# Seven products of 512 x 512 weights in two recurrent layers, each written as seven block products

## The chip, the cores and the metric

The kernel runs on one core of one Trainium2 chip. The time is the time of one execution on the device in microseconds (us). A core has five engines with queues of their own: TensorE (PE in the profile; PEld is its weight load), VectorE (DVE), ScalarE (ACT), GpSimd (POOL) and SyncE (SP), which issues most transfers (DMAs) between the memory of the chip (DRAM) and the core's on-chip memory. That on-chip memory is SBUF, 128 partitions wide, and PSUM, where TensorE puts its products, in banks of 128 x 512 numbers.

## What is computed

Four layers are applied in turn to x of shape (8, 112, 512): a cross attention (layer 0), two recurrent layers (1 and 2), and a layer with two attentions and an MLP (layer 3); layers 0 and 3 attend to a context of shape (8, 375, 512). All numbers are float32. The change lies in layers 1 and 2. Cut to what matters, layer 1 is:

```python
xa = _ln(x, ln1_w, ln1_b)
...                                     # r, k, v, g, w from mixes of xa and its shift by one token
def step(s, inp):
    k_l, v_l, w_l, r_l = inp
    a = k_l[..., :, None] * v_l[..., None, :]
    out = jnp.einsum('bhs,bhst->bht', r_l, faaaa * a + s)
    s_new = a + w_l[..., None] * s
    return (s_new, out)
_, outs = jax.lax.scan(step, s0, seq)   # over 112 tokens
y = outs.transpose(1, 0, 2, 3)
...                                     # group norm of y over each head
x = x + y * g @ Wo.T                    # time mix: the product called o
xc = _ln(x, ln2_w, ln2_b)
sxc = jnp.concatenate([state[:, i0][:, None], xc[:, :-1]], axis=1) - xc
xk2 = xc + sxc * fmaa_k
xr2 = xc + sxc * fmaa_r
rr = jax.nn.sigmoid(xr2 @ fWr.T)        # the product called fr
kk = jnp.square(jax.nn.relu(xk2 @ fWk.T))   # fk
x = x + rr * (kk @ fWv.T)               # channel mix: fv
```

Layer 2 has the same form, with weights Wfk, Wfr and Wfv. Everything in front of o is called the time mix, everything behind it the channel mix. All weights named here are 512 x 512.

## The kernel before

Activations lie transposed: 128 channels on the partitions, four channel blocks c, and 896 tokens along the row (8 sequences of 112), worked on in two halves h of 448 tokens. A tile of one activation is 128 x 4 x 896.

A product of such a tile with a weight is written in two ways:

- `project` (matmul at L167) makes, for each half h and each output block o, four matmuls of 128 x 128 by 128 x 448 over the four input blocks: 2 x 4 x 4 = 32 matmuls of 448 columns. In the profile one such matmul is two records. The function that is handed in takes each finished bank.
- `seven` (matmul at L1162) splits weight and activation into 2 x 2 blocks (two input and two output halves of 256 channels; two input halves by two token halves) and makes seven block products in place of eight: 7 x 2 input blocks x 2 output blocks m = 28 matmuls of 448 columns. It needs four sums of weight quarters (`weight_sums`, 128 x 512 each) and four sums of token blocks (`token_sums`, 128 x 896 each). Its parts have the names k1 to k8 in the tile names: k1 and k2 for both m first, and then for each m k6, k7, k5, k4 and k8, where k4 adds on to k7's bank and k8 to k5's. ACT copies k1 out (p1), DVE adds it to k6 (u2) and u2 to k7 (u3), and each output block is a bank plus u2 or u3. Layer 3 uses it for its queries, outputs and MLP, where the page calls its banks ps_k1q, ps_k6fc and so on.

In layers 1 and 2 the products o, fk, fr and fv go through `project`. Layer 3's keys and values do not depend on x. They are computed in layers 1 and 2 as a filler: `values()` hands out pieces (matmuls at L994), and `fill(n)` puts n pieces into PE's queue at places chosen by hand. ACT copies a piece out of PSUM (L1019, L1092, L1106), POOL adds parts together (L1020), SP loads the context's blocks (L978) and stores the result (L1010 to L1014), and POOL prepares sums of layer 3's value weights (L910 to L913, L930, L932).

The scan of the time mix (`time_mix`, L626) runs over 4 channel blocks of 16 steps each, 64 steps a layer, in this order: ACT copies v, spread to the partitions, into the PSUM buffer vp (L666, L667), DVE multiplies it by k into the PSUM buffer kv (L765), DVE scans with the decay into st (L769), POOL multiplies by r into rs (L773), and PE sums over the partitions (L746) when enough rs are there. vp and kv have one buffer each. The sums of a finished block are added to v's place (`take`, L712), which is now y, and its group norm (`group_norm`: reciprocals L699, POOL multiplies at L701 and, with the gate g, at L707) runs beside the scan of the next block; that of the last block runs behind the loop, beside filler. Then comes o, whose result is added to x by DVE (L794).

Inside the loop the order of the instructions on each engine is the order of the text (`tc.manual_schedule`). Around it, and in the channel mix, a scheduler chooses the order from dependencies, and may move an instruction that is written behind the loop into an engine's queue among the loop's.

The channel mix (L797) makes the shifted difference sxc (`shifted`, POOL, L437 and L438), mixes xk2 and xr2 from it (DVE, L819), and has `squared` as the end of fk (ACT relu L834, DVE square L835), a sigmoid on ACT at the end of fr (L844), and `add` at the end of fv (DVE product L850, POOL add L851). In layer 2, fv's second half of tokens is interleaved with layer 3's first LayerNorm.

## Time and profile before

| | us |
|---|---|
| three runs | 2889.84, 2891.95, 2893.08 |
| median | 2891.95 |
| profiled execution | 2892.85 |
| its span | 2890.7 |
| PE busy (97% of the span) | 2791.5 |
| DVE busy (62%) | 1800.7 |
| POOL busy (36%) | 1052.2 |
| ACT busy (35%) | 1012.7 |
| granted clock of PE, mean | 0.989 |

Times in the trace count from the start of the span; the execution's own time is 2.15 us more than the span. The scan loop of layer 1 runs from about 344 to 605, that of layer 2 from about 961 to 1226. o runs from 625 and from 1258, the channel mix's products from 697 to 767 and from 1344 to 1416. Busy shares are means over stages with different limits: the scan loops keep DVE and POOL busy as well as PE, the channel mixes keep PE alone busy.

An instruction's line in the timeline gives its start, its length, its engine, its line of the program, the operation, the tiles out<-in, the shapes and, in brackets, how long the engine was idle before and what released it. The chain of waits is the work that ended last, followed back from the end.

### The profile page before, as it was taken

What the parts mean: (1) busy time and instruction counts of PE and PEld (TensorE: products, weight loads), DVE (VectorE), ACT (ScalarE), POOL (GpSimd) and SP (SyncE); (2) the same over time, 40 slices, a digit from 0 to 9 for tenths busy, and PEclk for the clock granted to TensorE, in tenths of its full rate; (3) what the DMA queues carried; (4) which work ended last, traced back from release to release, by engine and by line L of the source; (5) the groups of instructions that cost most, each with busy time, mean ns of one, the idle gap of its engine ahead of it and who ended that gap; (6) DMA issues with size and microseconds to landing.
All of it is one profiled execution on the core that took longest, in us unless ns stands there. A gap on an engine that the chain in (4) does not pass through costs nothing.

```text
span 2890.7 us, 31049 instructions
## 1 busy us (share of the span) xinstructions
PE 2791.5 (97%) x10476; PEld 1588.2 (55%) x10476; DVE 1800.7 (62%) x2301; ACT 1012.7 (35%) x1953; POOL 1052.2 (36%) x836
## 2 busy tenths in 40 slices
PE   8989999999999999999999999999899999999999
PEld 4734443344444433347467676767476676767544
DVE  1464288856352688834457676757767676757555
ACT  2232466633243456523233232313333232313311
POOL 1432178744231487733322221313122232313030
PEclk9999999999999999999999999999999999999999
DMA  5621498944221789842435352525244352523010
GB/s 206 239 77 39 142 282 254 277 122 136 85 71 57 236 241 277 241 137 92 130 103 156 95 165 94 163 92 159 74 133 133 115 166 89 162 93 115 28 47 26
DMA packets 233310, 400.90 MB, mean 139 GB/s; under 512 B 35144, under 2 KB 170344, under 8 KB 226368
## 3 DMA queue, kind: packets, MB, share of 16 engines
q1 hardware_dynamic: 233152, 398.92, 44.1%
q8 instruction: 84, 1.38, 0.2%
q14 instruction: 74, 0.61, 0.1%
HBM read 321.06 MB, written 77.91 MB: 138 GB/s over the span
## 4 chain that ended last, share of the span: by engine, by line
PE 73%; DVE 15%; POOL 4%; ACT 4%; issue 2%; DMA 2%; SPq 0%; DVEq 0%; ACTq 0%; POOLq 0%
PE ps_vk L994 14%; PE ps_k1k L1235 8%; PE ps_k5k L1235 6%; PE av L1496 4%; PE sc L1448 4%; PE ps_o L167 3%; DVE each L1488 2%; PE ps_k1q L1162 2%; PE ps_fk L167 2%; PE ps_r L562 2%; PE ps_k L562 2%; PE ps_k5q L1162 2%; PE ps_k7q L1162 2%; PE ps_v L562 2%; PE ps_fr L167 2%
## 5 line engine op out<-in xcount | busy, mean ns | idle before, releaser
L994 PE MATMUL ps_vk<-wv,cv 128*128 128x512 f32 x1296 | 583.8, 601 | 15.4 <-ACT k L1092 9.1
L994 PEld LDWEIGHTS ps_vk<-wv,cv 128*128 128x128 f32 x1296 | 243.5, 191 | 339.8 <-issue 285.4
L1483 POOL PARTITION_ALL_REDUCE each<-tops x113 | 182.4, 1614 | 466.0 <-DVE tops L1472 464.1
L1020 POOL TENSOR_TENSOR k<-k,k 128x512 f32<-128x512 f32 (+1 forms) x153 | 197.8, 1293 | 327.0 <-ACT k L1019 276.4
L1458 POOL PARTITION_ALL_REDUCE tops<-top x128 | 139.3, 1088 | 427.5 <-DVE top L1456 417.3
L769 DVE TENSOR_TENSOR_SCAN st<-decay,kv 128x904 f32<-128x904 f32 x128 | 260.7, 2037 | 17.6 <-POOL rs L773 4.4
L773 POOL TENSOR_TENSOR rs<-st,r 128x896 f32<-128x896 f32 x128 | 247.3, 1932 | 51.6 <-DVE st L769 46.7
L1466 ACT ACTIVATE pts<-pts,rests 128x448 f32<-128x448 f32 (+1 forms) x256 | 133.2, 567 | 337.6 <-DVE pts L1464 325.9
L1496 PEld LDWEIGHTS av<-pts,v 125*128 125x128 f32 (+1 forms) x1536 | 190.9, 191 | 33.1 <-ACT pts L1466 3.9
L1448 PEld LDWEIGHTS sc<-q,k 128*128 128x128 f32 x1536 | 189.4, 192 | 33.0 <-DVE each L1488 9.4
L1448 PE MATMUL sc<-q,k 128*128 128x112 f32 x1536 | 193.0, 276 | 8.6 <-DVE each L1488 8.3
L1488 DVE RECIPROCAL each<-each 128x224 f32<-128x224 f32 x113 | 174.7, 1546 | 31.3 <-POOL each L1483 28.7
L1496 PE MATMUL av<-pts,v 125*128 125x112 f32 (+1 forms) x1536 | 190.9, 274 | 1.3 <-ACT pts L1466 1.3
L1235 PE MATMUL ps_k1k<-cs,wsk 128*128 128x375 f32 x480 | 173.6, 483 | 6.5 <-ACT u2k L1237 5.3
L765 DVE TENSOR_TENSOR kv<-vp,k 128x904 f32<-128x904 f32 x128 | 141.5, 1105 | 60.5 <-ACT vp L667 55.3
L1019 ACT COPY k<-ps_vk 128x512 f32<-128x512 f32 (+1 forms) x153 | 89.2, 583 | 179.6 <-PE ps_vk L994 176.8
L1092 ACT COPY k<-ps_vk 128x512 f32<-128x512 f32 (+1 forms) x153 | 89.1, 583 | 172.9 <-PE ps_vk L994 163.7
L1456 DVE TENSOR_REDUCE top<-sc 128x224 f32<-128x672 f32 x128 | 109.1, 852 | 28.6 <-PE sc L1448 28.6
L667 ACT COPY vp<-vj 128x896 f32<-128x896 f32 x124 | 112.8, 910 | 9.3 <-DMA vj<-rows 5.4
L1464 DVE TENSOR_TENSOR pts<-sc,tops 128x672 f32<-128x672 f32 x128 | 102.8, 803 | 17.6 <-POOL tops L1458 17.6
L1235 PEld LDWEIGHTS ps_k1k<-cs,wsk 128*128 128x128 f32 x480 | 84.0, 189 | 51.3 <-ACT u2k L1237 7.6
L1237 ACT COPY p1k<-ps_k1k 128x375 f32<-128x375 f32 x60 | 27.9, 465 | 212.1 <-PE ps_k1k L1235 212.1
(416 smaller groups left out, 4788.6 us busy)
## 6 DMA issues: line engine op xcount, KB each, us to landing
vj<-rows SPq DMA_DIRECT2D x124, 448.0 KB
cv<-blocks SPq DMA_DIRECT2D x181, 251.5 KB
cs<-blocks SPq DMA_DIRECT2D x120, 375.0 KB
wvs<-k SPq DMA_DIRECT2D x128, 256.0 KB
v<-wvs SPq DMA_DIRECT2D x128, 256.0 KB
cx<-in_ctxT SPq DMA_DIRECT2D x38, 750.0 KB
v<-wvs SPq DMA_DIRECT2D x128, 126.0 KB
wvs<-k SPq DMA_DIRECT2D x64, 224.0 KB
```

What stands on the lines that cost most here:

```text
L167: nc.tensor.matmul(p, w[:, k, o * P : (o + 1) * P], rhs(k, h), start=k == 0, stop=k == NC - 1)
L562: nc.tensor.matmul(y, ws[f][:, c, o * P : (o + 1) * P], x_f, start=c == 0, stop=c == NC - 1)
L769: nc.vector.tensor_tensor_scan(flat(st), flat(decay[:, c]), flat(kv), 0.0, ALU.mult, ALU.add)
L773: nc.gpsimd.tensor_mul(by_batch(rs), st[:, :, :L], by_batch(r[:, c, :]))
L994: nc.tensor.matmul(to, left, right, start=start and n == 0, stop=k == 1, skip_group_check=True)
L1020: nc.gpsimd.tensor_add(y, z, y)
L1162: nc.tensor.matmul(to, lhsT, rhs, start=start and k == 0, stop=k == 1, skip_group_check=not start)
L1235: nc.tensor.matmul(y, lhsT, rhs, start=start and k == 0, stop=k == 1, skip_group_check=True)
L1448: nc.tensor.matmul(sc[:, t, y * L : (y + 1) * L], kt[:, o, t * CT : t * CT + P], q[:, o, b * L : (b + 1) * L], start=True, stop=True,)
L1483: nc.gpsimd.partition_all_reduce(each, it[4], P, ReduceOp.add)
L1488: nc.vector.reciprocal(each, sums)
L1496: nc.tensor.matmul(av[:, y], v[:nt, t, y * HD : (y + 1) * HD], pts[:nt, t, y * L : (y + 1) * L], start=t == 0, stop=t == 2,)
```

## The change

o in both layers, fk and fr in both layers, and fv in layer 1 go from `project` to `seven`. fv of layer 2 stays.

- `weight_sums`, `token_sums`, `seven` and their helpers move up, so that layers 1 and 2 can call them. `seven` gets a switch `whole`, which writes k4 ahead of k5, and takes a function for the places of p1, u2 and u3.
- For o, the weight sums are made by DVE in the tile k, and the token sums by DVE in the tile r, in pieces of 128 x 448 (`sums_of_tokens`); the text has the calls behind the loop, in the last block's group norm. p1, u2 and u3 lie in the tile decay.
- For the channel mix, POOL makes the weight sums, in rr (fk), in sxc (fr), in sxc and xk2 (fv). DVE makes three token sums of 128 x 896 each and POOL the fourth. p1, u2 and u3 lie in a tile that LayerNorm has used before (tag "half"). xr2 has no tile any more: the mix is written over xc. A tile tx2 is new.
- fk's end becomes a DVE add (where there is u), a relu and a square on ACT. fr's gets a DVE add ahead of the sigmoid, fv's a DVE add ahead of the product, and o's second addend is added to x separately.

```diff
+    def weight_sums(pool, tag, w, u, eng=None, later=None):
...
+        a11, a12, a21, a22 = (w[:, k : k + 2, o : o + 256] for o in (0, 256) for k in (0, 2))
+        eng = eng or nc.gpsimd
+        steps = [
+            lambda: eng.tensor_add(y[0], a21, a22),
+            lambda: eng.tensor_sub(y[1], y[0], a11),
+            lambda: eng.tensor_sub(y[2], a11, a21),
+            lambda: eng.tensor_sub(y[3], a12, y[1]),
+        ]
+        if later is not None:
+            later.extend(steps)
+            return y
+        for step in steps:
+            step()
+        return y
+    def token_sums(eng, b11, b21, b12, b22, t):
+        eng.tensor_sub(t[:, 0], b12, b11)
+        eng.tensor_sub(t[:, 1], b22, t[:, 0])
+        eng.tensor_sub(b12, b22, b12)
+        eng.tensor_sub(t[:, 2], b21, t[:, 1])
+    def seven(ps, work, w, s, b, t, n, put, u, whole=False):
...
+        first, p1 = [], []
+        for m in range(2):
+            first.append(bank("k1", m))
+            product(first[m], m, lambda k: w[:, k], b11)
+            p1.append(tile_of("p1", m))
+            nc.scalar.copy(p1[m], first[m])
+            yield
+        for m in range(2):
+            product(first[m], m, lambda k: w[:, 2 + k], b21, start=False)
+            put(0, m, first[m], None)
+            yield
+        for m in range(2):
+            p = bank("k6", m)
+            product(p, m, lambda k: s()[1][:, k], t[1])
+            u2 = tile_of("u2", m)
+            nc.vector.tensor_add(u2, p, p1[m])
+            yield
+            p = bank("k7", m)
+            product(p, m, lambda k: s()[2][:, k], t[2])
+            u3 = tile_of("u3", m)
+            nc.vector.tensor_add(u3, p, u2)
+            yield
+            if whole:
+                product(p, m, lambda k: w[:, 2 + k, 256:], t[3], start=False)
+                put(0, 2 + m, p, u2)
+                yield
+            q = bank("k5", m)
+            product(q, m, lambda k: s()[0][:, k], t[0])
+            put(1, 2 + m, q, u3)
+            yield
+            if not whole:
+                product(p, m, lambda k: w[:, 2 + k, 256:], t[3], start=False)
+                put(0, 2 + m, p, u2)
+                yield
+            product(q, m, lambda k: s()[3][:, k], b22, start=False)
+            put(1, m, q, u2)
+            yield
+    def places(room, at, shapes):
+        room, ys = flat_all(room), []
+        for shape in shapes:
+            n = math.prod(shape)
+            y = room[:, at : at + n]
+            ys.append(y.rearrange("p (a b) -> p a b", b=shape[-1]) if len(shape) == 2 else y)
+            at += n
+        return ys
+    def temporaries(room, at=0):
+        a, b, c, e = places(room, at, [(NH,)] * 4)
+        given = {"p1": (a, b), "u2": (c, a), "u3": (e, e)}
+        return lambda what, m: given[what][m]
+    def quarters(y):
+        return [halves(y[:, k : k + 2], h) for h in range(2) for k in (0, 2)]
...
+            s_o = places(k, 0, [(2, 256)] * 4)
+            t_o = places(r, 0, [(2, NH)] * 3)
+            b11, b21, b12, b22 = quarters(y)
...
+            def sums_of_tokens(ks):
+                t0, t1, t3 = t_o
+                for k_ in ks:
+                    if not k_:
+                        for j in range(2):
+                            nc.vector.tensor_sub(t0[:, j], b12[:, j], b11[:, j])
+                    nc.vector.tensor_sub(t1[:, k_], b22[:, k_], t0[:, k_])
+                    nc.vector.tensor_sub(b12[:, k_], b22[:, k_], b12[:, k_])
+                    nc.vector.tensor_sub(t3[:, k_], b21[:, k_], t1[:, k_])
             last = group_norm(NC - 1, gate(NC - 1))
             for at in range(11):
                 next(last, None)
+                if not at:
+                    weight_sums(None, s_o, w_o, f"o{n}", nc.vector)
+                    sums_of_tokens([0])
                 fill(int(n == 2 or at % 2))
+            sums_of_tokens([1])
             banks.close()
             ps = banks.enter_context(tc.tile_pool(name=f"so{n}", bufs=6, space=PSUM))
-            def add(o, h, p):
-                xs = halves(x[:, o, :], h)
-                nc.vector.tensor_add(xs, p, xs)
-            project(ps, w_o, lambda c, h: halves(y[:, c, :], h), add, f"o{n}")
+            t0, t1, t3 = t_o
+            for _ in seven(
+                ps, temporaries(decay), w_o, lambda: s_o, (b11, b21, b22), (t0, t1, b12, t3), NH, add_to_x(None), f"o{n}", True
+            ):
+                pass
...
-            def mixed(maa, name):
-                y = one.tile([P, NC, N], F32, name=name)
+            def mixed(maa, y):
...
-            def squared(o, h, p):
+            def squared(h, o, p, u):
                 y = halves(kk[:, o, :], h)
+                if u is not None:
+                    nc.vector.tensor_add(y, p, u)
+                    p = y
                 nc.scalar.activation(y, p, AF.Relu)
-                nc.vector.tensor_mul(y, p, y)
-            xk = mixed(names["fk"], f"xk2_{n}")
-            project(ps, f_k, lambda c, h: halves(xk[:, c, :], h), squared, f"fk{n}")
-            xr = mixed(names["fr"], f"xr2_{n}")
-            project(
-                ps,
-                f_r,
-                lambda c, h: halves(xr[:, c, :], h),
-                lambda o, h, p: nc.scalar.activation(halves(rr[:, o, :], h), p, AF.Sigmoid),
-                f"fr{n}",
-            )
+                nc.scalar.activation(y, y, AF.Square)
+            def opened(h, o, p, u):
+                y = halves(rr[:, o, :], h)
+                if u is not None:
+                    nc.vector.tensor_add(y, p, u)
+                    p = y
+                nc.scalar.activation(y, p, AF.Sigmoid)
+            def sums_of(y, t):
+                b11, b21, b12, b22 = quarters(y)
+                t0, t1, t3 = t
+                nc.vector.tensor_sub(t0, b12, b11)
+                nc.vector.tensor_sub(t1, b22, t0)
+                nc.gpsimd.tensor_sub(b12, b22, b12)
+                nc.vector.tensor_sub(t3, b21, t1)
+                return (b11, b21, b22), (t0, t1, b12, t3)
+            def seven_of(w, s, y, t, put, u):
+                b, t = sums_of(y, t)
+                room = work.tile([P, NC, NH], F32, tag="half", name=f"parts_{u}")
+                weight_sums(None, s, w, u)
+                for _ in seven(ps, temporaries(room), w, lambda: s, b, t, NH, put, u, True):
+                    pass
+            xk = one.tile([P, NC, N], F32, name=f"xk2_{n}")
+            tx = one.tile([P, NC, N], F32, name=f"tx2_{n}")
+            s_k, s_r = (places(y, 0, [(2, 256)] * 4) for y in (rr, sx))
+            t_k, t_r = (places(y, 0, [(2, NH)] * 3) for y in (tx, xk))
+            mixed(names["fk"], xk)
+            seven_of(f_k, s_k, xk, t_k, squared, f"fk{n}")
+            mixed(names["fr"], xc)
+            seven_of(f_r, s_r, xc, t_r, opened, f"fr{n}")
...
+            def add7(h, o, p, u):
+                if u is not None:
+                    y = work.tile([P, NH], F32, tag="rstd", name=f"fvs{n}_{o}_{h}")
+                    nc.vector.tensor_add(y, p, u)
+                    p = y
+                add(o, h, p)
             if n == 1:
-                project(ps, f_v, lambda c, h: halves(kk[:, c, :], h), add, f"fv{n}")
+                s_v = places(sx, 2048, [(2, 256)] * 3) + places(xk, 2688, [(2, 256)])
+                seven_of(f_v, s_v, kk, t_k, add7, f"fv{n}")
```

## The prediction

> **What bounds the kernel now.** I read the page's busy shares and the engine shares of the chain first: TensorE (PE) is busy for 97% of the span. A microsecond of PE work saved is then a microsecond of time, if what feeds PE keeps up.
>
> ```profile
> PE 2791.5 (97%) x10476; PEld 1588.2 (55%) x10476; DVE 1800.7 (62%) x2301; ACT 1012.7 (35%) x1953; POOL 1052.2 (36%) x836
> PE 73%; DVE 15%; POOL 4%; ACT 4%; issue 2%; DMA 2%; SPq 0%; DVEq 0%; ACTq 0%; POOLq 0%
> ```
>
> The chain in order of time gives the price of the products that the change touches: PE waits for nothing inside them, and one matmul (two records) takes 24.05 / 32 = 0.75 us.
>
> ```profile
> 625.26 24.05 PE ps_o L167 x64
> ...
> 718.69 24.05 PE ps_fr L167 x64
> 742.74 24.07 PE ps_fv L167 x64
> ```
>
> The table by stretches (each "time, (instructions)" pair is PE, PEld, DVE, ACT, POOL) shows a stretch of the MLP, where products already run as seven blocks, beside a plain product and a stretch of the second scan loop.
>
> ```profile
> 2803.00:2824.00 21.00, 21.00 (x57) 10.64 (x56) 6.20 (x11) 5.67 (x9) 1.21 (x1) 1.00 0.11 45
> ...
> 718.00:742.00 24.00, 24.00 (x65) 12.14 (x64) 2.01 (x3) 7.53 (x11) 0.00 (x0) 1.00 0.12 44
> ...
> 1155.00:1224.00 69.00, 66.96 (x204) 27.39 (x202) 61.11 (x40) 40.25 (x75) 55.53 (x37) 1.00 0.84 243
> ```
>
> Seven blocks fill PE too (21.00 of 21.00). In the scan loop PE idles 2.04 of 69 us while DVE (61.11) and POOL (55.53) are nearly full: there, added DVE work has little room.
>
> **Part 1, fewer products.** Seven products fall from 32 matmuls to 28: 4 x 0.75 = 3.0 us each, 21.0 us in all, on the path. The extra adds from PSUM (0.62 us each) come at most five to a group of 7.5 us of PE work, as in the MLP: hidden.
>
> **Part 2, o's sums enter the scan loop.** In the built order of the changed kernel DVE does not take them behind the loop, where it sits idle for 12.37 us ahead of the reciprocals at 620.01. It takes four weight sums and five of the token sums in each layer between the loop's multiplies (kv) and scans. Three of those places wait for POOL's gate multiply of a finished channel block; the kv or scan behind waits along, then the vp copy on ACT (one PSUM buffer), then the filler's copies on ACT, whose banks PE needs. In the timeline of layer 2's last place (columns: start, us, engine):
>
> ```profile
> 1217.44 1.11 DVE L765 TENSOR_TENSOR kv<-vp,k 128x904 f32<-128x904 f32 x1
> 1218.65 2.04 DVE L769 TENSOR_TENSOR_SCAN st<-decay,kv 128x904 f32<-128x904 f32 x1
> 1220.90 1.11 DVE L765 TENSOR_TENSOR kv<-vp,k 128x904 f32<-128x904 f32 x1 [0.21 <-ACT vp L667]
> ...
> 1220.00 1.16 POOL L707 TENSOR_TENSOR v<-v,gate 128x448 f32<-128x448 f32 x1
> ...
> 1226.28 1.69 PE L746 MATMUL ps_y<-rs,pick 128*32 128x448 f32 x10 [1.02 <-POOL rs L773]
> ```
>
> The scan of 1218.65 now stands behind a sum that waits for the gate until 1221.16: it starts at 1221.8. Two more sums (1.2) put the last kv at 1225.1, its scan at 1226.3 to 1228.3, POOL's rs at 1228.4 to 1230.3 in place of 1226.2. PE already waits for it at 1226.28, so all 4.1 us count. Layer 1's last place:
>
> ```profile
> 598.63 1.14 POOL L707 TENSOR_TENSOR v<-v,gate 128x448 f32<-128x448 f32 x1
> ...
> 598.89 1.11 DVE L765 TENSOR_TENSOR kv<-vp,k 128x904 f32<-128x904 f32 x1 [0.15 <-ACT vp L667]
> ...
> 602.84 1.93 POOL L773 TENSOR_TENSOR rs<-st,r 128x896 f32<-128x896 f32 x1
> ...
> 604.82 1.69 PE L746 MATMUL ps_y<-rs,pick 128*32 128x448 f32 x10 [1.57 <-POOL rs L773]
> ```
>
> Gate until 599.77, three sums of 0.62, kv at 601.6, scan 602.8 to 604.85, rs at 604.85 instead of 602.84: 2.0 us.
>
> The sums may take longer than 0.62. Two inputs from SBUF, beside a busy POOL:
>
> ```profile
> 683.25 11.42 DVE L819 SCALAR_TENSOR_TENSOR xk<-sxc,vecs,xc 128x448 f32<-128x448 f32 x8
> 694.59 6.87 DVE L819 SCALAR_TENSOR_TENSOR xr<-sxc,vecs,xc 128x448 f32<-128x448 f32 x8
> ```
>
> The same operation takes 1.43 us each while POOL works without a pause (680.99 to 693) and 0.86 beside two POOL adds. The kv and scan rows, with one input in PSUM, keep 1.11 and 2.04 whatever POOL does. If each sum stands behind the POOL operation that is then running, the first one of layer 1 starts at 601.67, after an rs: 3.9 us there, and in layer 2 an add until 1222.4 and an rs until 1227.0 make 7.2. I take a middle: 3.0 (2.0 to 3.9) and 5.5 (4.1 to 7.2).
>
> [...]
>
> The four earlier places, by the same reading:
> - Layer 1, kv of 468.39: the gate ends at 472.38, kv starts at 473.0, 4.6 late. POOL is behind there (its next rs for this block starts only at 477.76), so the scans' sums are not later. But the vp copy of 469.99 waits until 474.1, and the filler's copies on ACT behind it with it; PE has one product of 1.72 us in hand and gives back 0.7 that it idled at 479.75: 4.1 - 1.7 - 0.7 = 1.7 (0 to 4.6).
> - Layer 1, second place: kv of 534.51 goes to 536.0, less than a product: 0.3 (0 to 1.5).
> - Layer 2, kv of 1086.35: gate until 1089.18, kv 3.5 late, vp copy 2.7 late, less one product: 1.0 (0 to 3.5).
> - Layer 2, scan of 1154.22: gate until 1156.71, 3.1 late: 0.9 (0 to 3.1).
>
> The eight weight sums (0.6 each) fall between scans, where DVE has short idle times: 1.0 (0 to 4.8). Part 2 together: 13.4 us (6.1 to 28.6).
>
> **Part 3, o itself.** Its last gate multiply (630.56) is done by about 631.3, k6 starts 8 matmuls after 625.2, at 631.2; five adds to x are 3.1 us in 7.5: nothing (0 to 1).
>
> **Part 4, the channel mixes.**
> - fk of layer 1: DVE's mixing of xk ends at 694.6; three sums of 1.1 and eight mixes of 0.67 end at 703.3, or at 709 with a POOL operation ahead of each of four. Of fk's records 58 ran from 696.89; k1 and k2 would end at 700.6, k6 at 702.1, k7 and k5 at 705.1, and k4 cannot start before u3, two adds behind k6 on DVE: 1.5 (0 to 5).
> - fr's sums on DVE stand between the adds of fk's second half, two of 1.1 us ahead of adds that PE waits for: 0.7 in each layer, 1.4 (0 to 5).
> - fr of layer 1: on POOL seven weight sums (1.27 each) and the four wv sums (705.08 to 714.7 before, 2.35 each) now stand ahead of the token sum that k7 reads; 704 + 8.9 + 9.4 + 1.9 = 724.2, while k7 starts at about 725: 0.5 (0 to 3).
> - fk of layer 2: POOL's four weight sums of fr wait for the mixing and stand ahead of the filler's last four adds (L1020, 1334.09 to 1344.93); ACT has two buffers for these, and PE's pieces of 1339 to 1344 can wait: 1.0 (0 to 4).
> - Entry to layer 2: four POOL adds close together at fv's end, yet the load of Wv that the chain shows from 766.83 on starts some 3 us earlier against that end: 0 (-1 to 2).
> - ACT does the square: eight operations of 0.54 us more in each layer; ACT has 7.53 us of work in the 24 of 718 to 742: nothing (0 to 1, if its copies of p1 come late). No DMA is added.
>
> Part 4: 4.4 (-1 to 19).
>
> **Sum.** -21.0 + 13.4 + 0 + 4.4 = -3.2. The profiled run took 2892.85 (span 2890.7 and 2.15 around it), 0.90 above the median of 2891.95: 2889.65 for such a run, 2888.75 at the median, so 2889.
>
> **Rivals.** A measurement of this kernel tells 0.2% (5.8 us) from no change: the runs before spread over 3.2 us.
> - Absorbed: the loop's delays vanish in PE's own idle time (3.95 us of 1024 to 1090, 2.04 of 1155 to 1224) and in part 4 nothing shows. For it: DVE idles 3.52 at 1086.35, just where a sum goes. Against it: the last places end in a PE that already waits. -21 + 6.1 + up to 3 gives 2877 (2871 to 2880).
> - Slower, by one mechanism: sums with two SBUF inputs collide with POOL wherever they stand. At the last places that is 3.9 + 7.2, at the earlier ones one operation of POOL (1.3 to 1.9) ahead of each, some 4 x 1.5 more on the 3.9 taken, 8 weight sums at 1.4 rather than 0.6 (6), and the upper values for both fk, 9. Together 21.0 - 36 = 15 over; it decides from about 27 us of loss. 2898 to 2907. For it: the 11.42 us row. Against it: rows beside a sparse POOL (0.86).
> - The loop costs as in my sum, but the channel mixes wait for their sums, mostly the POOL queue ahead of k7 and the filler's adds: 10 to 19 instead of 4.4, 2894 to 2903.
>
> That seven blocks do not save 3.0 us each is hardly open, with 21.00 of 21.00 in the MLP.
>
> **Numbers.** My sum, with 2880 to 2897 as its own range: 0.37 (half of it under 2886.2). Absorbed 0.23, collisions 0.28, late sums 0.12 (about half within 0.2%). Faster 0.18 + 0.23 = 0.41, same 0.19 + 0.07 = 0.26, slower 0.28 + 0.05 = 0.33. The range reaches from the middle of the absorbed case to inside the collisions: 2874 to 2904.
>
> **What will show it.** Seven groups of 56 records at 21.0 us instead of 64 at 24.05; in the loops DVE sums that wait for POOL's gate multiplies, the scans behind them late, and PE waits for the last rs of 3 to 8 us instead of 1.57 and 1.02; sums of 128x448 longer than 0.62 where POOL is busy; PE gaps ahead of k4 in fk and k7 in fr. I am wrong if the stretches of the scan loops keep their length, or if a gap of over 5 us stands somewhere else, ahead of layer 2's first LayerNorm above all.

## The result: slower by 34.5 us, and the profile after

The changed kernel takes 2925.40 us (median of four runs, 2924.47 to 2931.13) against 2890.89 us of the kernel before on the same chip (four runs, 2889.32 to 2893.08). The ratio is 1.0121 with a 95% interval of 1.0109 to 1.0133: slower by 34.5 us. The prediction was 2889 (2874 to 2904). The profiled execution is the slowest of the four: 2931.13, with a span of 2929.0, 38.3 over the 2890.7 of before. All stage times below are from that execution.

The busy shares and the engine shares of the chain on the page of the changed kernel:

```profile
PE 2790.1 (95%) x10420; PEld 1585.8 (54%) x10420; DVE 1893.2 (65%) x2394; ACT 1029.4 (35%) x1983; POOL 1101.9 (38%) x861
PE 69%; DVE 17%; POOL 5%; ACT 4%; issue 3%; DMA 2%; SPq 1%; DVEq 0%; POOLq 0%; ACTq 0%
```

PE has 56 records fewer (28 matmuls of 0.75 us, 21 us), but its busy time falls by 1.4 us only, and its mean granted clock falls from 0.989 to 0.982: matmuls have become longer elsewhere. DVE has 92.5 us more to do and POOL 49.7. Their shares of the chain went up from 15% to 17% and from 4% to 5%.

Where the 38.3 us arise is read by putting the starts and ends of the same instructions of both profiles side by side. The table gives the offset of after against before at each mark, and what each stretch added:

| mark (time in before, us) | offset | the stretch up to it |
|---|---|---|
| first scan of layer 1 (347.08) | +2.32 | nothing is changed here |
| last scan of layer 1 (600.10) | +15.15 | scan loop: +12.83 |
| o starts (625.09) | +17.47 | rs, PE's wait, last block: +2.32 |
| o ends (649.31) | +16.30 | o as seven: -1.17 |
| fk starts (685.37) | +17.07 | LayerNorm: +0.77 |
| fk ends (718.69) | +23.97 | fk as seven: +6.90 |
| fr ends (742.74) | +21.26 | fr as seven: -2.71 |
| fv ends (766.80) | +19.98 | fv as seven: -1.28 |
| first scan of layer 2 (965.22) | +23.98 | entry to layer 2: +4.00 |
| last scan of layer 2 (1222.11) | +37.47 | scan loop: +13.49 |
| o starts (1258.12) | +39.03 | as above: +1.56 |
| o ends (1282.33) | +36.03 | o as seven: -3.00 |
| fk starts (1319.98) | +38.16 | LayerNorm: +2.13 |
| fk ends (1365.99) | +43.17 | fk as seven: +5.01 |
| fr ends (1390.04) | +40.17 | fr as seven: -3.00 |
| end (2890.74) | +38.25 | fv of layer 2, layer 3: -1.92 |

The two time mixes up to o cost 30.2 us, the two fk 11.9 where 6.0 were to be saved, the entry to layer 2 4.0. Only o of layer 2 and fr bring their 3 us. fv's blocks run without a pause as well, but 1.72 us of filler stand among them now.

The chain of waits of the changed kernel at the end of layer 1's loop (start, length, engine, tile, line):

```profile
605.46 1.92 POOL rs L914
607.38 1.23 POOL k L1206
608.61 1.10 POOL v L845
...
609.73 2.33 DVE r L933
612.05 1.62 DVE v L934
613.67 0.53 DVE r L935
614.20 1.03 DVE kv L906
...
615.25 2.05 DVE st L910
...
617.47 1.92 POOL rs L914
...
619.43 3.19 PE ps_y L887 x10
```

This is the row to compare with before's 598.63 to 604.82. POOL's gate multiply (L845) comes behind an rs and a filler add. Three token sums of o (L933 to L935) wait for it in DVE's queue, and the layer's last kv and scan stand behind them. On the chain two of the sums take 2.33 and 1.62 us, the third 0.53. PE waits 6.25 us for the last rs (1.57 in before). The same place in layer 2, in the timeline (in brackets the idle time before, and what ended it):

```profile
1252.13 1.67 DVE L933 TENSOR_TENSOR r<-v,r 128x448 f32<-128x448 f32 x1 [2.62 <-POOL v L845]
1256.19 2.33 DVE L935 TENSOR_TENSOR r<-v,r 128x448 f32<-128x448 f32 x1
1263.75 3.19 PE L887 MATMUL ps_y<-rs,pick 128*32 128x448 f32 x10 [4.72 <-POOL rs L914]
```

PE had idled 1.92 us just before that, so 6.6 us in all (1.02 in before). And what follows such a pause is slow as well. The table by stretches (time, then PE, PEld, DVE, ACT and POOL busy with their instructions, then the granted clock of PE, the DMA share and GB/s) shows the time behind three of the pauses:

```profile
619.40:622.60 3.20, 3.17 (x11) 0.60 (x11) 0.00 (x0) 0.00 (x0) 0.00 (x0) 0.50 0.00 0
622.60:631.00 8.40, 8.40 (x18) 3.74 (x18) 1.09 (x1) 1.75 (x3) 2.18 (x2) 0.84 0.26 76
...
726.70:730.10 3.40, 3.36 (x5) 1.72 (x6) 0.62 (x1) 1.15 (x2) 3.40 (x3) 0.50 0.00 0
...
1384.20:1388.00 3.80, 3.73 (x17) 3.73 (x18) 0.00 (x0) 0.02 (x1) 1.81 (x2) 0.50 0.73 270
```

Behind pauses of 6.25, 4.51 and 3.94 us the granted clock is 0.50. It is back at 1.00 at 625.3, 731.1 and 1389.9, which is 4.4 to 5.9 us after the matmuls go on (3.3 us behind the pause of layer 2's loop). At this clock the ten ps_y matmuls take 3.19 us, in before 1.69. Each of these pauses so cost its own time and, by an estimate from these times, some 1.6 to 2.9 us more: half of the time at the low clock.

In fk of layer 1 (timeline, DVE and PE):

```profile
718.75 6.67 DVE L973 SCALAR_TENSOR_TENSOR xc<-sxc,vecs,xc 128x448 f32<-128x448 f32 x6
725.35 0.61 DVE L334 TENSOR_TENSOR parts_fk<-ps_k6fk,parts_fk 128x448 f32<-128x448 f32 x1
726.74 3.35 PE L305 MATMUL ps_k7fk<-tx,w_L_xattn_fWk_None 128*128 128x448 f32 x4 [4.51 <-DVE parts_fk L339]
734.54 2.61 DVE L1004 TENSOR_TENSOR xk<-xc 128x896 f32<-128x896 f32 x1
737.60 2.69 DVE L1005 TENSOR_TENSOR xk<-xc,xk 128x896 f32<-128x896 f32 x1
737.74 1.77 PE L305 MATMUL ps_k7fk<-tx,w_L_xattn_fWk_None 128*128 128x448 f32 x4 [1.05 <-DVE parts_fk L339]
740.89 1.77 PE L305 MATMUL ps_k5fk<-xk,rr 128*128 128x448 f32 x4 [1.38 <-DVE kk L989]
```

The scheduler has put all eight mixes of fr (the last six are the first row) ahead of fk's first add (u2) in DVE's queue, while k6 had ended at about 719. k4 (the matmuls of 726.74, which add on to k7's bank) waits for DVE, and then so do k4 and k8 of the other m, behind two token sums of fr. Pauses of 4.51 + 1.05 + 1.38 = 6.94, and two pieces at the low clock (3.35 and 2.08 us for what takes 1.50): 9.4 of the 9.9 us that separate +6.90 from -3.0.

In fk of layer 2 the wait comes through POOL:

```profile
1376.40 1.58 POOL L273 TENSOR_TENSOR sxc<-w_L_xattn_Wfr_None 128x512 f32<-128x512 f32 x1 [2.88 <-DVE xc L973]
...
1382.38 3.63 POOL L1206 TENSOR_TENSOR k<-k,k 128x500 f32<-128x500 f32 x3
1383.64 0.58 ACT L1205 COPY k<-ps_vk 128x500 f32<-128x500 f32 x1 [5.45 <-POOL k L1206]
1384.27 3.78 PE L1180 MATMUL ps_vk<-cv,wv 128*128 128x125 f32 x16 [3.94 <-ACT k L1205]
```

fr's four weight sums wait for DVE's mixing of fr (they overwrite sxc), and stand ahead of the filler's adds. ACT's copies have two buffers, PE's filler has its banks, and k1's second half stands behind the filler in PE's queue. 3.94 of pause, 1.07 of a later one, and 2.7 at the low clock make 7.7 of the 8.0 us lost.

### The profile page after: what moved, and what is told of

Read it like the earlier page. It is cut to its first block, busy times and chain, and to the rows that moved or that the text cites. A ratio compares the mean times of both kernels' runs of the same rounds, so it can differ in the third digit from the quotient of the medians.

```text
span 2929.0 us, 31116 instructions
## 1 busy us (share of the span) xinstructions
PE 2790.1 (95%) x10420; PEld 1585.8 (54%) x10420; DVE 1893.2 (65%) x2394; ACT 1029.4 (35%) x1983; POOL 1101.9 (38%) x861
## 4 chain that ended last, share of the span: by engine, by line
PE 69%; DVE 17%; POOL 5%; ACT 4%; issue 3%; DMA 2%; SPq 1%; DVEq 0%; POOLq 0%; ACTq 0%
PE ps_vk L1180 12%; PE ps_k1k L1329 8%; PE ps_k5k L1329 6%; PE av L1573 4%; PE sc L1525 4%; DVE each L1565 2%; PE ps_k5o L305 2%; PE ps_k7o L305 2%; DVE st L910 2%; PE ps_k L700 2%; PE ps_r L700 2%; PE ps_k5q L305 2%; PE ps_k7q L305 2%; PE ps_v L700 2%; PE ps_k1q L305 2%
## 5 line engine op out<-in xcount | busy, mean ns | idle before, releaser
L906 DVE TENSOR_TENSOR kv<-vp,k 128x904 f32<-128x904 f32 x128 | 141.3, 1104 | 48.5 <-ACT vp L805 42.5
L1533 DVE TENSOR_REDUCE top<-sc 128x224 f32<-128x672 f32 x128 | 109.1, 853 | 28.6 <-PE sc L1525 28.6
L1541 DVE TENSOR_TENSOR pts<-sc,tops 128x672 f32<-128x672 f32 x128 | 102.8, 803 | 17.6 <-POOL tops L1535 17.6
```

Of the source, the lines that this page charges most:

```text
L906: nc.vector.tensor_mul(flat(kv), flat(vp), flat(k[:, c]))
```

## The experiments

Theory L: the loop's losses come from instructions of DVE that wait for POOL's gate multiplies, and from nothing else that o's change does. Theory K: in the channel mixes, DVE's and POOL's work for fr stands in front of what PE waits for in fk; the products themselves do gain 3 us each. Rivals: the added DVE time alone (weight sums), seven blocks that are slow here, or one part on which all hangs.

### Which part costs: o alone, and the mixes alone

In the first, the channel mixes are those of before; in the second, o is.

```diff
 # o alone: channel_mix() as before the change
-            seven_of(f_k, s_k, xk, t_k, squared, f"fk{n}")
+            project(ps, f_k, lambda c, h: halves(xk[:, c, :], h), squared, f"fk{n}")
...
 # the mixes alone: time_mix() as before the change
-                if not at:
-                    weight_sums(None, s_o, w_o, f"o{n}", nc.vector)
-                    sums_of_tokens([0])
...
-            sums_of_tokens([1])
...
+            project(ps, w_o, lambda c, h: halves(y[:, c, :], h), add, f"o{n}")
```

> Only the two o go through seven blocks, with their sums where the changed kernel has them; the channel mixes are those of the kernel before. Theory A (the sums that DVE takes between the scans cost most): the profiles' difference by stage is +14.0 us for layer 1's time mix and +12.0 for layer 2's, o's own saving included, so +26 us against the kernel before (22 to 29). Theory B (the channel mixes lose most of it, and a late loop is made up for behind it): at most +8 us.

> Only the five products of the channel mixes go through seven blocks, o stays a plain product. Theory A: +3.7 (mix of layer 1) + 4.0 (entry to layer 2) + 2.3 (mix of layer 2) = +10 us against the kernel before (6 to 13); with o alone it adds up to the whole change's +34.5 within 4 us. Theory B: +26 us or more.

o alone takes 2919.35 us, 1.0102 (1.0087 to 1.0118) of before, +29.5. The mixes alone take 2903.18, 1.0045 (1.0029 to 1.0060), +13. In the profiles the two offsets at the end, 29.0 and 8.4, add up to 37.4 against 38.3 of both together; the ratios make 42.5 against 35.0, so a difference between whole executions should not be read closer than some 4 us. Both parts lose, each nearly alone responsible for its own stages: with o alone the stretches up to o give +14.8 and +17.9, with the mixes alone +2.4 and -2.3. Of the expectations o's loss was above the range and the mixes' was at its upper end.

### The loop's loss: token sums kept behind the loop

The text that follows the loop goes into the block in which each engine keeps the order of the text, so that nothing of it can be put between the last kv's and scans.

```diff
             with tc.manual_schedule(engines=ORDERED):
...
-            last = group_norm(NC - 1, gate(NC - 1))
-            for at in range(11):
...
-            sums_of_tokens([1])
+                last = group_norm(NC - 1, gate(NC - 1))
+                for at in range(11):
...
+                sums_of_tokens([1])
```

> The changed kernel with its text order kept up to o: the same sums, on the same engine, but all behind the last scan, in the stretch where DVE was idle for 12.4 us. Theory A: the loops' +12.8 and +13.5 go, and with them the slow clock behind their last wait (about 3 us once or twice): 34.5 - 26.3 - 3 = +5 us against the kernel before (0 to 9). Theory C (the sums cost wherever they stand, since group norm and o wait for them): +15 us or more.

This takes 2903.20 us, 1.0051 (1.0034 to 1.0068). The loops' losses are gone: +0.6 in layer 1 (0.99 to 1.63) and -1.1 in layer 2 (11.34 to 10.24). That part of the expectation held. The total did not: +14.7 is about what the mixes alone cost, so o still gains nothing. All engines now follow the text behind the loop, and in layer 1 o starts 4.3 us late. In layer 2 o takes 26.3 us, more than the 24.2 of `project`. Its timeline shows why (the first row is the same kind of sum with POOL idle):

```profile
1244.46 0.61 DVE L934 TENSOR_TENSOR v<-v 128x448 f32<-128x448 f32 x1
...
1269.49 2.36 POOL L1136 TENSOR_TENSOR wv<-wx 128x1024 f32<-128x1024 f32 x1
1269.58 2.75 DVE L933 TENSOR_TENSOR r<-v,r 128x448 f32<-128x448 f32 x1 [12.10 <-POOL v L845]
1271.93 2.61 POOL L1138 TENSOR_TENSOR wx<-wx,wx 128x1024 f32<-128x1024 f32 x1
...
1281.74 3.29 PE L305 MATMUL ps_k7o<-r,w_L_xattn_Wo 128*128 128x448 f32 x4 [3.12 <-DVE decay L339]
```

The three last sums take 2.75 us each in place of 0.61, about as long as the POOL operations of 2.4 to 2.6 beside them. 8.3 us instead of 1.8 stand ahead of o's adds on DVE, and PE waits.

### The wait or the work: weight sums in the loop, token sums behind

Both kernels are o alone, and only DVE's order is kept behind the loop. In the first the four weight sums are free to go into the loop; in the second POOL makes the last three token sums.

```diff
+            weight_sums(None, s_o, w_o, f"o{n}", nc.vector)      # first kernel only
+            with tc.manual_schedule(engines={mybir.EngineType.DVE}):
...
                 for at in range(11):
                     next(last, None)
                     if not at:
-                        weight_sums(None, s_o, w_o, f"o{n}", nc.vector)   # first kernel only
                         sums_of_tokens([0])
...
-                sums_of_tokens([1])                              # second kernel only
+                sums_of_tokens([1], nc.gpsimd)
```

> Only the two o go through seven blocks. The four weight sums stay among the scans, as in the changed kernel; the token sums, which wait for POOL's gate multiplies, stand behind the loop on DVE. Theory A1 (it is the waits for the gate that cost): each loop is at most 2 us longer than before, against 12.8 and 13.5. Theory A2 (any work that DVE takes in the loop counts): four of nine sums, some 5.5 us a loop. The whole time by A1: layer 1 -3 + 2, layer 2 -3 + 5 (its last three sums stand beside POOL's sums of layer 3's weights, 2.75 us each in the run with the sums behind the loop) = +1 us (-3 to +5); by A2 +8 or more.

> Only the two o go through seven blocks. All sums behind the loop: weight sums and the first five token sums on DVE, the last three token sums on POOL, so that they meet no other POOL work. Theory E (the pause inside layer 2's o, 3.1 us and slow matmuls behind it, is the collision of DVE's last sums with POOL): o takes 21 to 22 us in both layers, the loops keep their length, and the time is -4 us against the kernel before (-6 to 0). Theory C (sums behind the loop cost the start of o as much as they save): 0 to +5 us.

With the weight sums alone in the loops these grow by 0.9 and 1.5 us instead of 12.8 and 13.5: it is the token sums that cost, not the four weight sums a layer. What part of that is their wait for the gate and what part their own length beside POOL, these runs do not separate. In layer 1 of the changed kernel DVE waits 4.12, 1.07 and 1.06 us for the gate at the three places, and the token sums there take 2.33, 2.34 and 4.6. The whole takes 2894.03, 1.0019 (1.0009 to 1.0029), some 4 us above what was expected: o gains 1.2 and 3.0, but the profiled execution (2890.39) is the fastest but one of eleven, and shows no place for the rest of the median.

With POOL's sums it is 2886.67, 0.9991 (0.9982 to 1.0000): -2.6 us, inside the -6 to 0 that was expected, and hardly clear of no change. o of layer 2 now runs its 28 matmuls in 21.2 us without a pause. o of layer 1 gains 1.2 us. The timeline (ACT, PE) shows the wait that is left there, and that after has too:

```profile
629.62 0.76 ACT L841 ACTIVATE v<-v,gn 128x448 f32<-128x448 f32 x1 [2.61 <-POOL v L839]
630.29 0.94 ACT L324 COPY decay<-ps_k1o 128x448 f32<-128x448 f32 x2
630.86 3.27 PE L305 MATMUL ps_k1o<-v,w_L_xattn_Wo 128*128 128x448 f32 x8 [1.57 <-ACT decay L324]
```

k2 adds on to k1's bank, so it waits until k1 is copied to p1; the copy stands on ACT behind a group norm step of the last half, which waits for POOL.

### The channel mixes: which product loses

First fk is a plain product, with fr and fv as in the change and o as before. Then fv is plain too, and fr's weight sums are made by POOL, as in the change, or by DVE.

```diff
 # all three: o as before, and
-            seven_of(f_k, s_k, xk, t_k, squared, f"fk{n}")
+            project(ps, f_k, lambda c, h: halves(xk[:, c, :], h), squared, f"fk{n}")
 # the second and third: also
-                seven_of(f_v, s_v, kk, t_k, add7, f"fv{n}")
+                project(ps, f_v, lambda c, h: halves(kk[:, c, :], h), add, f"fv{n}")
 # the third: also
-                weight_sums(None, s, w, u)
+                weight_sums(None, s, w, u, nc.vector)
```

> As the channel mixes alone, but fk stays a plain product in both layers (with its square on DVE); fr in both layers and fv in layer 1 go through seven blocks, their sums made while fk runs. Theory A': fk is what loses in the channel mixes, 10.0 us of pauses and slow matmuls in layer 1 and some 6.5 in layer 2 against 6.0 saved: +10 - 16.5 + 6 = about 0 us against the kernel before (-4 to +3). Theory D (the loss lies in the late end of fv and the entry to layer 2, or in POOL's queue): +7 us or more.

> Only fr in both layers goes through seven blocks, weight sums on POOL as in the changed kernel; o, fk and fv are plain products. Layer 1: -3.0, and no late entry to layer 2 (the 4 us there come from fv as seven blocks). Layer 2: fk keeps its pause, since POOL's weight sums stand ahead of the filler's adds: +5.9 - 3.0. Together 0 us against the kernel before (-2 to +2). If the entry to layer 2 is late whatever fv does: +4 us.

> As fr with POOL's weight sums, but DVE makes them. Theory F (fk of layer 2 pauses because the filler's adds stand behind POOL's weight sums): the pause goes, both fr save 3.0: -6 us against the kernel before (-7 to -3). Rival (the pause comes from DVE's mixing and the token sums beside it): as with POOL, within 1.5 us.

They take 2891.25, 1.0005 (0.9996 to 1.0015); 2891.20, 1.0010 (1.0001 to 1.0019); and 2887.78, 0.9995 (0.9986 to 1.0004). fr itself gains 3.0 us in each layer of all three. But in the first two, fk of layer 2, a plain product now, is 5.9 and 6.0 us longer than in before. That is the whole of fr's gain in both layers, so fk's loss there is fr's, by POOL's queue. The first kernel's time was the expected one, but its reason was not, since fk was held to lose by itself. With the sums on DVE fk is 2.1 longer. By its execution times the third kernel gains 1.4 us, where 6 were expected, and cannot be told from no change; its profiled execution ends 6.1 earlier than that of before, but that one, with 2892.85, lies 1 to 4 us above the medians that before had in these series (2888.53 to 2891.82). What is left of fk's loss, in the timeline of the third kernel:

```profile
1334.20 0.68 DVE L273 TENSOR_TENSOR sxc<-w_L_xattn_Wfr_None 128x512 f32<-128x512 f32 x1
1334.42 6.21 POOL L987 TENSOR_TENSOR xc<-xc 128x896 f32<-128x896 f32 x1 [4.01 <-DVE tx L985]
```

Now POOL is the one that is slowed: its single token sum takes 6.21, where an rs of the same shape takes 1.93. DVE does five more sums of two inputs in that time, one right behind the other, the last from 1338.01 to 1338.69; 1.93 later POOL is done. The filler's adds stand behind it.

fv as seven made no measurable difference: with it and without it the ratios overlap. In the profile with it, PE's wait at the next LayerNorm is 1.89 us and a later one 2.61 (none and 0.45 in before), and the granted clock is 0.91 over the 39 us from the end of fv on (1.00 in before). The changed kernel has the same two waits and the same 0.91:

```profile
786.81 0.62 DVE L1039 TENSOR_TENSOR fvs<-ps_k5fv,parts_fv 128x448 f32<-128x448 f32 x1 [0.99 <-PE ps_k5fv L305]
788.49 1.60 DVE L188 TENSOR_TENSOR part_mean_ln<-x 128x448 f32<-128x448 f32 x1
792.10 1.37 PE L192 MATMUL mean_ln<-part_mean_ln,mean_c 128*128 128x448 f32 x2 [1.89 <-DVE part_mean_ln L190]
812.11 1.02 PE L663 MATMUL ps_t<-xx,maa 128*128 128x448 f32 x2 [2.61 <-DVE xx L654]
```

`project` finishes the first half of the tokens 12 us before its end, and LayerNorm's partial sums for it are done beside the second half. `seven` finishes the last block of both halves at its end (k4 and k8 of m = 1), so all of LayerNorm starts there. Not all of the late entry need be fv's: up to layer 2's first scan it is 3.8 to 4.3 us longer than in before in the four kernels with fv as seven, but in the eight with a plain fv it also lies between 0.2 shorter and 2.7 longer.

### Versions that keep the gains

The first: o with POOL's last sums, p1 copied by DVE, and fr with all its sums on DVE; fk and fv plain. The second adds fk as seven in both layers, with DVE's order written out, one step of fr's mixing and sums behind each part of fk. The third does that for fk in layer 2 only.

```diff
 # first, to o alone with POOL's last sums
-            nc.scalar.copy(p1[m], first[m])
+            copy(p1[m], first[m])                       # nc.vector.tensor_copy for o
...
-                nc.gpsimd.tensor_sub(b12, b22, b12)
+                nc.vector.tensor_sub(b12, b22, b12)
 # second (both layers) and third (layer 2)
+                weight_sums(None, s_k, f_k, f"fk{n}")
+                with tc.manual_schedule(engines={mybir.EngineType.DVE}):
+                    for step in mixed(names["fk"], xk) + sums_of(xk, t_k):
+                        step()
+                    steps = mixed(names["fr"], xc) + sums_of(xc, t_r)
+                    weight_sums(None, s_r, f_r, f"fr{n}", nc.vector, steps)
+                    for at, _ in enumerate(seven_of(f_k, s_k, xk, t_k, squared, f"fk{n}")):
+                        for step in steps[:1]:
+                            step()
+                        del steps[:1]
```

> Both o and both fr as seven blocks, fk and fv plain. o's sums behind the loop (last three on POOL), p1 of o copied by DVE instead of ACT, all of fr's sums on DVE. If the causes found so far are the whole of it (waits in the loop, p1 behind the group norm on ACT: 1.6 us in layer 1, two-input sums of DVE and POOL that hold each other up: POOL's sum of 128x896 took 6.21 us in the run with DVE's weight sums, and fk of layer 2 paused 2 us for it), each of the four products saves 3.0 us: -12 us against the kernel before (-13 to -8). If the savings of o and fr do not add up, or new waits come: -2.3 - 1.2 = -4 us as the two runs measured alone.

> As the run with o and fr, and fk too as seven blocks in both layers, with DVE's order written out: fk's token sums, then one mix or sum of fr after each step of fk's product; fk's weight sums on POOL early, all else on DVE. If DVE's order was fk's fault, fk saves up to 3.0 us more in each layer: -14 us against the kernel before (-18 to -10). If DVE simply has too much in that stretch: fk loses again some 3 to 6 us a layer, -4 us or worse.

> Both o, both fr, and fk of layer 2 alone as seven blocks; fk of layer 1 and both fv plain. In the run with both fk, layer 1's lost 2.8 us (fk 36.1 us after the stages before instead of 33.3) where POOL's sums of layer 3's weights (2.35 us each before, 2.6 to 3.1 there) held DVE's two-input sums for 2.2 to 2.7 us; layer 2's, with POOL idle, saved 3.0 (stage by stage -5.50 to -8.50). If that collision is the whole difference: 2.8 us less than with both fk by the stages' ends, no pause over 2 us in fk of layer 2, and -13 us against the kernel before by the clock (-16 to -8). If fk's saving in layer 2 needs the late layer 1: no better than o and fr alone.

The first takes 2884.25, 0.9973 (0.9964 to 0.9981), -6 to -8 us where -12 was expected: each of its four products gains its 2.5 to 3.0 us (11.5 in all), but not all of it arrives at the end. Part of it is seen to be lost in stretches that no edit touches, such as a wait of 2.26 us ahead of ps_ruk in layer 2 (0.58 in before); why it comes is open.

The second takes 2882.11, 0.9975 (0.9964 to 0.9985), short of the -10 to -18 us that were expected. fk of layer 2 gains its 3.0, but fk of layer 1 takes 4.1 more than the plain product, a loss of 7.1 against 9.9 in the changed kernel:

```profile
703.70 2.24 DVE L973 SCALAR_TENSOR_TENSOR xc<-sxc,vecs,xc 128x448 f32<-128x448 f32 x1
709.10 2.70 DVE L1007 TENSOR_TENSOR rr<-xc 128x896 f32<-128x896 f32 x1
715.54 3.25 PE L305 MATMUL ps_k7fk<-tk,w_L_xattn_fWk_None 128*128 128x448 f32 x4 [5.05 <-DVE parts_fk L339]
```

The written order has only one step of fr ahead of each of fk's adds, but POOL makes the value weights' sums (four of 2.6 to 3.1 us) from 702.77 to 714.00, and DVE's steps take 2.24 to 2.70 in place of 0.67 and 1.08. So the order in DVE's queue was the smaller part of this loss.

The third, without that one product, takes 2874.24 us (2873.18 to 2877.81, five runs) against 2891.82 (nine runs): 0.9943 (0.9929 to 0.9956), 17.6 us faster than before and 51 faster than the changed kernel. Its two o, two fr and second fk gain 2.6 to 3.0 each, 14.5 in all; the other 3 us come in stretches without an edit, and are within what such stretches drift from run to run (the second scan loop is 2.7 shorter than in before, in the first of these kernels 0.5). Its page:

```profile
PE 2775.5 (97%) x10436; PEld 1580.0 (55%) x10436; DVE 1855.3 (65%) x2377; ACT 1025.2 (36%) x1975; POOL 1066.2 (37%) x846
PE 73%; DVE 15%; ACT 4%; POOL 4%; issue 2%; DMA 2%; SPq 0%; DVEq 0%; ACTq 0%; POOLq 0%
```

PE has 16 us less of work than in before, and the shares of the chain are those of before: no other engine has moved onto it.

## Why the prediction was wrong

The mechanisms were named, and most sizes were too small. By its own steps, with the losses on top of -3.0 a product (each stretch of the table, corrected by 3.0 where it holds a product):

| step | predicted | profiled |
|---|---|---|
| part 1, fewer products | -21.0 | -21.0 |
| part 2, loops and wait for the last rs | +13.4 (6.1 to 28.6) | +15.2 and +15.1 = 30.2 |
| part 3, o itself | 0 (0 to 1) | +1.8 in layer 1, 0 in layer 2 |
| part 4, fk of layer 1 with fr's sums in it | +2.2 | +9.9 |
| part 4, fk of layer 2, the same | +1.7 | +8.0 |
| part 4, fr of layer 1 | +0.5 | +0.3 |
| part 4, fv and the entry to layer 2 | 0 (-1 to 2) | +5.7 |
| LayerNorms between o and fk | none | +2.9 |
| sum | -3.2 | +37.8 |

With +2.3 that stand already ahead of the first loop and -1.9 behind layer 2's fr, which no step explains, this is the 38.3.

**Part 1** held: seven blocks take 21.0 us wherever their inputs are there (o of layer 2 in 21.2, fr in 21.05).

**Part 2** failed first, and the step that failed is the rebate. At the four earlier places the kv or scan was found 1.5 to 4.6 late, 12.7 us in all, but only 3.9 of it were counted: POOL was held to be behind anyway, one filler product to be in hand, and PE to have idle time of its own. The trace after shows the lateness kept to the end of the loop. Layer 1's first place in the timelines (DVE), before and then after:

```profile
469.60 2.04 DVE L769 TENSOR_TENSOR_SCAN st<-decay,kv 128x904 f32<-128x904 f32 x1
...
468.57 2.04 DVE L910 TENSOR_TENSOR_SCAN st<-decay,kv 128x904 f32<-128x904 f32 x1
474.73 2.33 DVE L932 TENSOR_TENSOR r<-v 128x448 f32<-128x448 f32 x1 [4.12 <-POOL v L845]
478.11 2.04 DVE L910 TENSOR_TENSOR_SCAN st<-decay,kv 128x904 f32<-128x904 f32 x1
```

The scan of 478.11 is the one of 469.60 in before; a token sum that waited for the gate stands ahead of it and its kv. The intervals between the starts of scans tell the rest. Where nothing holds it, a scan follows the last after 3.35 us in before, and kv (1.11) and scan (2.04) with their starts make just that; twelve intervals in each layer hold a reciprocal of 1.53 besides (4.58 and more). From this place on the intervals are 3.35, 4.70, 5.43, 3.35, 4.14 in before and 9.54, 6.37, 3.35, 3.35, 4.14 in after: 2.1 us are made up at once, and 5.8 stay. In 50 of the 63 intervals of layer 1 and in 48 of layer 2, DVE idles less than 0.35 us in before; there DVE sets the pace and the others follow it, so a delay of DVE is a delay of the loop. The share of 61.11 in 69 us hid this, being a mean over stretches with DVE full and the changes from block to block. The four earlier places so cost 5.8 and 1.7 in layer 1, 4.9 and 2.2 in layer 2, instead of 1.7, 0.3, 1.0 and 0.9; the weight sums that stand beside them are in these figures. With the weight sums alone the two loops grew by 0.9 and 1.5, 2.4 together against 1.0 in the sum. At the last places, +5.2 and +6.5 come before the scan, against 3.0 and 5.5 in the sum: four of the six token sums took 1.67 to 2.33 us against 0.62.

**A term that the sum did not have** is the clock. Every pause was priced at its length. Behind the four pauses of 3.9 to 6.6 us the granted clock was 0.50, and this cost some 1.6 to 2.9 us each, 9 to 10 us in all, and some 3 more at the entry to layer 2. The prediction had expected pauses of 3 to 8 us, and before's own profile has a stretch at 0.50 (685.96 to 689.37, behind a pause of 2.79), so the term could have been there. Behind these four pauses the clock is 0.50 for 3.3 to 5.9 us of work, then 1.00; the shorter ones are told of in the last section.

**Part 3** overlooked that p1's copy stands behind the group norm on ACT: 1.57 us of pause, in the kernel with POOL's sums as in after. It goes where DVE copies p1 (o of layer 1 then gains 2.5).

**Part 4** had the right waits in fk of layer 1 and took sizes near the low end. It let DVE's mixes end between 703.3 and 709 and counted 1.5 (0 to 5) for k4. They ended at 725.42 in a kernel whose fk starts 17.07 later, which is 708.4 in before's time, and k4's pause was 4.51. fr's two token sums, at 2.61 and 2.69 us in place of 1.1, made pauses of 1.05 and 1.38 where 0.7 was counted, and the low clock added 2.4. The written order took only 2.8 of the 9.9 us away. In fk of layer 2 the step that failed is the wait that was waived: the filler's adds were seen to come late, but PE's pieces "can wait". They stand ahead of k1 in PE's queue, and cannot. (The upper end of part 4 adds up to 20, not 19, which changes nothing.) That fr's weight sums on POOL do this alone is shown by the two kernels with a plain fk: +5.9 and +6.0. For the entry to layer 2 the sum saw four adds close together, but not that all of LayerNorm moves behind them. That is the reading of the trace; no run changes the order of fv alone, and part of the 5.7 us may be drift, since kernels with a plain fv had up to 2.7 there.

**The rivals.** "Absorbed" is refuted by the offsets that stay. "Collisions" is the mechanism that runs through the steps that grew (sums of 2.3 to 2.8 in place of 0.6 to 1.1), and its sign was right, but its 2898 to 2907 is short of 2925, because it also let the loop absorb part of the delays and did not know of the clock. "Late sums in the mixes" was right in kind, at 24 us with the entry instead of 10 to 19. The chances were given as if these cases excluded each other; the last two came together.

## What to carry to other kernels

Before work is added to an engine, look in each stretch for what sets its pace, by the interval between the same instructions, not by the busy share: a delay put into that chain stayed to the end of the loop here, with 5.8 of 7.9 us at layer 1's first place. Ask for each added instruction what it waits for and what stands behind it in the same queue, where the scheduler chooses the order above all, and count with a slow stretch behind a pause of TensorE: the granted clock was 0.50 behind six pauses of 1.89 to 6.6 us in the changed kernel, which cost an estimated 1.5 to 2.9 us each, and stayed at 1.00 behind one of 2.81 in before. The saving itself was real: with waiting sums kept out of the loop, sums on the engine that is free at that time, and products left plain where DVE and POOL are both full, five of the seven products kept their 14.5 us, in a kernel whose median is 17.6 us lower.

## What the runs showed of the hardware

In these runs DVE sums of two SBUF inputs and POOL operations took longer beside each other. A DVE sum of 0.61 us took 2.75 beside POOL operations of 2.4 to 2.6 (o's last sums, kept behind the loop), one of 1.08 took 2.70 beside POOL's of 2.62 and 3.07 (fk of layer 1 in the second of the versions that keep the gains), and the other way round a POOL sum took 6.21 beside a row of DVE sums, where an rs of its shape takes 1.93. Operations with an input in PSUM kept their times: fk's adds 0.61 between those POOL operations of 2.62 and 3.07, kv 1.08 to 1.11 and the scan 2.02 to 2.04 in all 128 of each in after, also where POOL was busy throughout. For sums that each stand behind the POOL operation that is then running, the prediction had 3.9 and 7.2 at the two last places. The profile has 5.2 and 6.5, and the middle that it took, 3.0 and 5.5, was the wrong choice. New is the row of 6.21: it ends 1.93 behind the last of several DVE sums that ran one after the other.

The clock was not expected to fall behind short pauses. At the entry to layer 2 it is 0.50 from 792.57 to 795.98, behind a pause of 1.89 us, and from 813.05 to 816.46, behind one of 2.61. In before it stays at 1.00 behind one of 2.81 (831.47 to 834.28). In the traces of both kernels every stretch at 0.50 within the span is 3.41, 6.83 or 10.24 us long, and the starts of these stretches lie whole multiples of 3.41 apart: here the clock went in steps of 3.41. The table by stretches (PE busy is the second time), cut at these steps, after and then before:

```profile
789.15:792.57 3.42, 1.53 (x5) 0.49 (x3) 3.32 (x6) 2.42 (x4) 0.67 (x3) 1.00 0.73 193
792.57:795.98 3.41, 3.41 (x6) 1.40 (x5) 3.13 (x3) 1.84 (x3) 1.27 (x1) 0.50 0.58 114
...
829.32:832.74 3.42, 2.15 (x5) 0.60 (x4) 0.46 (x1) 3.33 (x6) 0.00 (x0) 1.00 0.45 142
832.74:836.15 3.41, 1.87 (x6) 0.60 (x6) 1.41 (x3) 1.83 (x3) 0.00 (x0) 1.00 0.18 68
```

In after, 1.89 us of idle time fall into one step, and the next step is low. The longer pause of before is split over two steps, with 1.27 and 1.54 in each. In these two traces, from 220 us on, a low step came behind each of the 20 full-speed steps in which PE idled 1.94 us or more, and behind three of the five with 1.89 to 1.91. It came behind none with less, except near 270 and 900 us, where PE runs matmuls of 32 rows (0.26 to 0.62 us idle). So it mattered here how much of a pause fell into one step, not its length alone. Nor was the step ahead of a low one always idle as a whole: in that of 789.15, PE was busy for 1.53 of 3.42 us.
